# Making the transposed activations of two packs from a transposed input instead of on TensorE

## The chip, the cores and the metric

The kernel runs on one core of a Trainium2 chip. The metric is the device time of one execution in microseconds, here the median of three runs. One further execution was recorded by the hardware profiler; all the views below come from it. The core has TensorE (PE, matrix products and transposes), VectorE (DVE), ScalarE (ACT), GpSimd (POOL) and SyncE (SP), which here only issues DMA transfers.

## The reference

Two graph layers are applied to x (3327 rows of 512 features) with one weighted adjacency matrix, all in fp32. Each layer begins with a layer norm over each row, and a relu:

```
h = jnp.maximum(_layernorm(x, axis=-1), 0.0)
x = x + _L0_gnn_ref(h, adj, adj, Wq, bq, Wk, bk, Wv, bv)   # softmax(q k^T / sqrt(512) + 2 adj) v
h = jnp.maximum(_layernorm(x, axis=-1), 0.0)
x = x + _L1_gnn_ref(h, adj, W)                              # normalised adjacency, twice
```

The layer norm is (x - mean) / sqrt(variance + 1e-5), with no learned scale or offset. Because the scale of a row is positive, relu((x - mean) * rstd) equals max(x - mean, 0) * rstd. The change concerns only h of the first layer, in the stage that makes the queries.

## The kernel before, in words

The rows are padded to 26 tiles of 128. In most of the kernel the products are formed by a seven-product scheme for 2 x 2 blocks, so operands are kept as blocks and as sums of blocks. The first stage, which takes about the first 116 us, forms M = Wq^T Wk (scaled), the normalised h, its transpose, and the projection of the transposed h by M, which is stored to DRAM (`qd`) and read back by the score stage.

The 13 pairs of row tiles (tile t of the upper half and tile t of the lower half) are cut into four packs, `PACKS = ((0, 4), (4, 3), (7, 3), (10, 3))`, and the packs are worked in the order `TURN = (1, 2, 0, 3)`. Pack 0 has four pairs, so its products have 512 columns; the others have three pairs and 384 columns.

`h_transposed(k)` takes the pack's tiles one by one. `load_x` brings a tile of x from DRAM on SP's queue. `norm` computes mean and variance with bn_stats and bn_aggr on VectorE (L194, L196), adds epsilon (L198), and GpSimd raises the sum to the power -0.5 (L200, `rstd`); VectorE makes the bias -mean * rstd (L204). ScalarE applies relu(x * rstd + bias) (L323), which gives `ht`. SP stores `ht` to DRAM for later stages (L324). TensorE transposes it in four blocks of 128 x 128 into a PSUM bank of `tp` (L327). ScalarE copies the blocks into `hp[k]` (L330 for a tile of the upper half, L332 for two blocks of a lower one), and VectorE forms the block sums that need the other two blocks straight from PSUM (L333, L334). Once the pack is complete VectorE forms two more sums over all its columns (L335, L336).

`hp[k]` thus has seven parts, each of two blocks: part 0 is used by product m1, 1 by p2, 2 by p4, 3 by p5, 4 by p6, 5 by p7 and 6 by p3. The mapping is the dictionary `A`.

`project_q(k)` runs two `Chain`s, one for each half of the output features. A chain issues its seven products in the order m1, p5, p2, p6, (the p4 that the chain before left open), p3, p7 into PSUM banks X, Y and Z. ScalarE evicts some of the results into `qs` (L352), VectorE adds others to `qs` (L355), and after the second chain SP stores the four `qs` tiles to `qd` (L362). There is one set of `qs` tiles for all packs, so the next pack's evictions wait for those stores.

The order on each engine in this stage is not written out by hand: a scheduler places the instructions by its own estimate of readiness, and each engine then runs its list in that order. In the stage after it, the order is pinned by `in_order`. In the first stage the scheduler lays the transposes of a pack between the products of the pack ahead of it. The x tiles lie in a ring of eleven buffers and the `ht` tiles in a ring of four.

Of the kernel before, what the change touches and what calls it, by code (L numbers as in the profile page):

```python
# [35 lines left out]
HALF = 13  # L36
# [7 lines left out]
ROW = tuple(STRIPS[s] + y * HT[s] + k for y in range(2) for s in range(2) for k in range(HT[s]))  # L44
# [3 lines left out]
def graph_layers_kernel(  # L48
    ctx: ExitStack,
    tc: tile.TileContext,  # L50
    x: bass.AP,
    adjT: bass.AP,
    wq: bass.AP,
    wk: bass.AP,
# [22 lines left out]
    nc = tc.nc  # L77
    N = out.shape[0]
    NP, D = x.shape
    DC = D // P  # L80
    NT = NP // P
    scale = 1.0 / math.sqrt(D)
# [17 lines left out]
    def large(k, shape, name):  # L100
        return arena.tile(shape, F32, name=name, tag=f"large{k}")
# [4 lines left out]
    def half(k, shape, name):  # L106
        return arena.tile(shape, F32, name=name, tag=f"half{k}")

    def bank(k, name):
        return banks.tile([P, BW], F32, name=name, tag=f"bank{k}")  # L110

    def ring(*slots):

        turn = itertools.cycle(slots)

        def take(shape, name):
            kind, k = next(turn)
            return kind(k, shape, name)

        return take  # L120
# [18 lines left out]
    dram = ctx.enter_context(tc.tile_pool(name="dram", bufs=1, space=bass.MemoryType.DRAM))  # L139
    small = ctx.enter_context(tc.tile_pool(name="small", bufs=4))  # L140

    ident = const.tile([P, P], F32, name="ident")
# [23 lines left out]
    totd = dram.tile([1, NP], F32, name="totd")  # L166
    x1d = [dram.tile([P, D], F32, name=f"x1d{i}") for i in range(NT)]
    rowd = [[dram.tile([P, D], F32, name=f"row{g}_{i}") for i in range(NT)] for g in range(3)]
    t2d = [[dram.tile([P, 4, P], F32, name=f"t2{g}_{t}") for t in range(PAIRS + 1)] for g in range(3)]

    def four_sums(o, g):
# [16 lines left out]
        lo, hi = max(r0, c0), min(r0 + P, c0 + a.shape[-1])  # L188
        return (slice(lo - c0, hi - c0), ident[:, lo - r0 : hi - r0]) if lo < hi else None

    def norm(src):

        st = small.tile([P, 6], F32, name="st")
        nc.vector.bn_stats(st, src)  # L194
        mv = small.tile([P, 2], F32, name="mv")
        nc.vector.bn_aggr(mv, st)  # L196
        ve = small.tile([P, 1], F32, name="ve")
        nc.vector.tensor_scalar(ve, mv[:, 1:2], EPS, None, op0=ALU.add)  # L198
        rstd = small.tile([P, 1], F32, name="rstd")
        nc.gpsimd.tensor_tensor(rstd, ve, mhalf, op=ALU.pow)  # L200

        def bias():
            nb = small.tile([P, 1], F32, name="nb")
            nc.vector.scalar_tensor_tensor(nb, mv[:, 0:1], -1.0, rstd, op0=ALU.mult, op1=ALU.mult)  # L204
            return nb

        return rstd, bias
# [17 lines left out]
    def psum_ring(*ks):  # L225
        turn = itertools.cycle(ks)
        return lambda name: bank(next(turn), name)

    x_bank, y_bank, z_bank, tp_bank = psum_ring(0, 1), psum_ring(2, 3), psum_ring(4, 5), psum_ring(6, 7)
# [40 lines left out]
    x_ring = ring(*((mid, k) for k in range(6, 15)), (half, 13), (half, 14))  # L270
    n_ring = ring(*((mid, k) for k in range(4)))

    def load_x(i, queue=nc.sync):
        xt = x_ring([P, D], "xt")
        queue.dma_start(xt, x[ROW[i] * P : (ROW[i] + 1) * P])
        return xt

    order = [(k, t + y * HALF) for k in TURN for t in range(PACKS[k][0], sum(PACKS[k])) for y in range(2)]
# [29 lines left out]
    for r in range(DC):  # L308
        for z in range(2):
            turned = -scale if r < 2 and z == 0 else scale  # L310
# [5 lines left out]
    def h_transposed(k):  # L316

        a, n = PACKS[k]
        for _, i in (o for o in order if o[0] == k):
            xt = first.pop(i) if i in first else load_x(i)  # L320
            rstd, bias = norm(xt)
            ht = n_ring([P, D], "ht")
            nc.scalar.activation(ht, xt, AF.Relu, bias=bias(), scale=rstd)  # L323
            nc.sync.dma_start(rowd[0][ROW[i]], ht)  # L324
            pt = tp_bank("tp").rearrange("p (c e) -> p c e", c=DC)
            for c in range(DC):
                nc.tensor.transpose(pt[:, c], ht[:, c * P : (c + 1) * P], ident)  # L327
            w = slice((i % HALF - a) * P, (i % HALF - a + 1) * P)
            if i < HALF:
                nc.scalar.copy(hp[k][:, 0:2, :, w], pt.rearrange("p (a c) e -> p a c e", a=2))  # L330
            else:
                nc.scalar.copy(hp[k][:, 2, :, w], pt[:, 2:4])  # L332
                nc.vector.tensor_add(hp[k][:, 3, :, w], hp[k][:, 2, :, w], pt[:, 0:2])  # L333
                nc.vector.tensor_add(hp[k][:, 5, :, w], hp[k][:, 0, :, w], pt[:, 0:2])  # L334
        nc.vector.tensor_add(hp[k][:, 4], hp[k][:, 3], hp[k][:, 0])  # L335
        nc.vector.tensor_add(hp[k][:, 6], hp[k][:, 1], hp[k][:, 4])  # L336

    def project_q(k):
        a, n = PACKS[k]
        w = n * P  # L340

        qs = [half(8 + j, [P, 2, BW], "qs") for j in range(4)]

        def chain(o):
            def product(ps, name, start):
                for c in range(2):
                    nc.tensor.matmul(ps[:, :w], M[B[name]][:, c, o * P : (o + 1) * P], hp[k][:, A[name], c],  # L347
                                     start=start and c == 0, stop=c == 1, skip_group_check=True)

            def first(j, ps, sign):  # L350
                d = 2 * (j % 2) + o
                nc.scalar.activation(qs[j][:, o, :w], ps[:, :w], AF.Identity, bias=u[:, d : d + 1], scale=float(sign))  # L352

            def more(j, ps):
                nc.vector.tensor_add(qs[j][:, o, :w], qs[j][:, o, :w], ps[:, :w])  # L355

            def last():
                if o == 1:
                    for j in range(4):
                        y, z = divmod(j, 2)  # L360
                        i = ROW[y * HALF + a] * P
                        nc.sync.dma_start(qd[:, 2 * z : 2 * z + 2, i : i + w], qs[j][:, :, :w])  # L362

            Chain(product, first, more, last)

        for o in range(2):
            chain(o)
# [5 lines left out]
            nc.tensor.matmul(pu[:, r : r + 1], w_k[c // 2][:, c % 2, r * P : (r + 1) * P], bq_sb[:, c : c + 1],  # L373
                             start=c == 0, stop=c == DC - 1)
    nc.vector.tensor_scalar(u, pu[:, :DC], scale, None, op0=ALU.mult)
    for k, then in itertools.zip_longest(TURN, TURN[1:]):
        if then is not None:
            h_transposed(then)
        project_q(k)

# [144 lines left out]
    def beside_of(k):  # L525
        def on(j, what, *args):
            if 0 <= j < len(steps):
                getattr(pairs[j], what)(*args)

        def difference():  # L530
            if k < len(steps) and steps[k][1] >= 6:
                next(more_of, None)

        return (
            lambda: (on(k - 2, "s4"), on(k - 2, "gather", 0)),
            lambda: (on(k - 1, "s3"), on(k - 2, "gather", 1)),
            lambda: on(k + 1, "sum_of_adjacency", 0),
            lambda: on(k + 1, "sum_of_adjacency", 1),
            lambda: (on(k - 2, "total", 0), difference()),
            lambda: (on(k - 2, "total", 1), on(k - 1, "s1")),  # L540
            lambda: on(k - 1, "s2"),
        )
# [9 lines left out]
    with in_order(*(e.engine for e in (nc.vector, nc.tensor, nc.gpsimd, nc.sync))):  # L552
        for k, (n, t) in enumerate(steps):
# [116 lines left out]
    parts = {}  # L670
# [147 lines left out]
    class Gather:  # L818
# [14 lines left out]
        def parts(self, of):  # L833

            return [of[k][:, w] for k, w in self.spots]
# [40 lines left out]
    def where(i):  # L876

        s = int(i >= STRIPS[1])
        return (s, *divmod(i - STRIPS[s], HT[s]))
# [142 lines left out]
    def number_of(g, r, s, t):  # L1022
        return ((g * len(ORDER) + r) * 2 + s) * len(every) + t
# [18 lines left out]
    for n, job in enumerate(jobs):  # L1042
        k = k0 + n * (k1 - k0) // len(jobs)
# [15 lines left out]
    k = number_of(0, 5, 1, 2)  # L1059
# [16 lines left out]
    for (n, s, t), its in {  # L1076
# [15 lines left out]
    k = number_of(1, 4, 0, 0)  # L1092
# [480 lines left out]
```

## Time and profile before

| | us |
|---|---|
| runs shown, median of 3 | 2179.59 (2177.32 to 2180.01) |
| the profiled execution | 2178.22 |
| span of its instructions | 2176.4 |
| TensorE busy in the span | 2163.2 (99%) |
| VectorE busy | 1664.5 (76%) |
| ScalarE busy | 238.4 (11%) |
| GpSimd busy | 49.0 (2%) |
| TensorE's transposes of h (L327), busy | 16.4 |
| the products of `project_q` end, first products of the score stage | about 116 to 122 after the start |

The span is the time from the first to the last instruction. Busy time counts an engine as busy while at least one of its instructions runs; matmuls overlap, so the mean length of one is longer than the distance between two starts. In a group of instructions, what stands after the second bar is the idle time of the engine just before them and what ended it. Lines such as L327 are lines of the kernel before; where the text speaks of operations that only the changed kernel has, it goes by the names in the diff.

### The profile page before, as it was taken

How to read it: one execution, taken by the hardware profiler on the slowest of the kernel's cores; microseconds unless marked ns; L12 is line 12 of the kernel's file. 1: busy time of each engine (PE TensorE's matmuls, PEld its weight loads, DVE VectorE, ACT ScalarE, POOL GpSimd, SP SyncE). 2: the span in 40 equal slices, each digit the busy share in tenths (PEclk: the TensorE clock that was granted, in tenths of full speed). 3: DMA queues.
4: the chain of work that ended last, by engine and by line, in shares of the span. 5: the costliest groups of instructions: out<-in, count | busy, mean ns of one | idle time of the engine just before them, and what ended most of it. 6: DMA issues, size and time to landing. Idle time of an engine off the chain costs nothing.

```text
span 2176.4 us, 21093 instructions
## 1 busy us (share of the span) xinstructions
PE 2163.2 (99%) x6424; PEld 1197.1 (55%) x6424; DVE 1664.5 (76%) x3250; ACT 238.4 (11%) x363; POOL 49.0 (2%) x60
## 2 busy tenths in 40 slices
PE   9999999999999999999999999999999999999998
PEld 6555555455555555555454555555666655555555
DVE  6369888888886698886778778887676667778686
ACT  5312111121110000000000000000011100000011
POOL 2000000000000000000111000000000000000000
PEclk9999999999999999999999999999999999999999
DMA  8568888889989899888787889986646468756685
GB/s 290 177 222 308 294 298 287 294 290 310 321 290 298 291 377 331 287 296 304 259 304 263 308 277 370 320 303 219 207 145 200 142 202 276 254 188 212 218 305 194
DMA packets 300374, 583.68 MB, mean 268 GB/s; under 512 B 34518, under 2 KB 168028, under 8 KB 300252
## 3 DMA queue, kind: packets, MB, share of 16 engines
q1 hardware_dynamic: 265102, 512.76, 69.4%
q10 hardware_dynamic: 35150, 69.48, 8.7%
q8 instruction: 53, 0.87, 0.2%
q14 instruction: 69, 0.57, 0.1%
HBM read 414.28 MB, written 167.85 MB: 267 GB/s over the span
## 4 chain that ended last, share of the span: by engine, by line
PE 95%; DVE 3%; DMA 1%; issue 1%; ACT 0%; POOL 0%; DVEq 0%; POOLq 0%
PE p L813 54%; PE Y L454 13%; PE Z L454 7%; PE p L805 5%; PE p L905 4%; PE pw L966 3%; PE X L454 3%; PE Y L347 2%; PE Z L347 1%; PE mm L306 1%; DMA part<-sum 1%; PE tp L327 1%; DVE part L173 1%; PE pt L995 1%; PE X L347 0%
## 5 line engine op out<-in xcount | busy, mean ns | idle before, releaser
L813 PE MATMUL p<-part,b 128*128 128x448 f32 (+1 forms) x3528 | 1261.5, 513 | 0.3 <-DVE part L174 0.2
L813 PEld LDWEIGHTS p<-part,b 128*128 128x128 f32 x3528 | 668.1, 190 | 534.7 <-issue 284.7
L454 PE MATMUL Y<-qt,hp 128*128 128x448 f32 (+1 forms) x832 | 308.2, 513 | 0.3 <-DVE g L466 0.3
L173 DVE TENSOR_TENSOR part<-part 128x896 f32<-128x896 f32 (+1 forms) x252 | 257.0, 1020 | 65.7 <-DMA part<-p 24.0
L454 PEld LDWEIGHTS Y<-qt,hp 128*128 128x128 f32 x832 | 157.7, 190 | 134.3 <-issue 72.3
L454 PE MATMUL Z<-qt,hp 128*128 128x384 f32 (+1 forms) x416 | 162.5, 513 | 0.0
L175 DVE TENSOR_TENSOR part<-part,part 128x448 f32<-128x448 f32 (+1 forms) x219 | 129.5, 591 | 14.9
L174 DVE TENSOR_TENSOR part<-part,part 128x448 f32<-128x448 f32 (+1 forms) x219 | 129.4, 591 | 7.2
L805 PE MATMUL p<-part,b 128*128 128x448 f32 (+1 forms) x336 | 124.2, 513 | 0.0
L454 PEld LDWEIGHTS Z<-qt,hp 128*128 128x128 f32 x416 | 78.8, 190 | 67.4 <-issue 37.2
L458 DVE SCALAR_TENSOR_TENSOR g<-g,Y 128x384 f32<-128x384 f32 (+1 forms) x156 | 91.5, 587 | 31.3 <-PE Y L454 28.6
L805 PEld LDWEIGHTS p<-part,b 128*128 128x128 f32 x336 | 63.7, 190 | 53.5 <-issue 31.2
L841 ACT COPY part<-p 128x384 f32<-128x384 f32 (+1 forms) x33 | 16.6, 502 | 657.5 <-PE p L813 542.1
L454 PE MATMUL X<-qt,hp 128*128 128x384 f32 (+1 forms) x208 | 81.1, 512 | 0.0
L461 ACT ACTIVATE g<-g 128x768 f32<-128x768 f32 (+1 forms) x48 | 43.0, 896 | 347.8 <-DVE g L458 278.6
L905 PE MATMUL p<-w,ct 128*128 128x512 f32 x136 | 61.8, 594 | 0.5 <-DVE part L917 0.5
L842 DVE TENSOR_TENSOR part<-p,part 128x384 f32<-128x384 f32 (+1 forms) x33 | 19.3, 585 | 51.6 <-PE p L813 50.9
L454 PEld LDWEIGHTS X<-qt,hp 128*128 128x128 f32 x208 | 39.5, 190 | 33.1 <-issue 19.3
L200 POOL TENSOR_TENSOR rstd<-ve,mhalf 128x1 f32<-128x1 f32 x52 | 43.0, 830 | 567.9 <-DVE ve L198 538.7
L966 PE MATMUL pw<-w,rows 128*128 128x256 f32 x208 | 53.6, 380 | 0.8 <-DVE rows L956 0.8
L896 DVE TENSOR_TENSOR job<-job 128x896 f32<-128x896 f32 (+1 forms) x52 | 52.9, 1018 | 0.0
L466 DVE TENSOR_TENSOR g<-g,Z 128x384 f32<-128x384 f32 (+1 forms) x52 | 30.5, 586 | 26.8 <-PE Z L454 26.4
(176 smaller groups left out, 1697.6 us busy)
## 6 DMA issues: line engine op xcount, KB each, us to landing
part<-sum SPq DMA_DIRECT2D x104, 448.0 KB, 5.0
part<-p SPq DMA_DIRECT2D x91, 448.0 KB, 6.0
part<-sum SPq DMA_DIRECT2D x104, 384.0 KB, 3.7
part<-p SPq DMA_DIRECT2D x91, 384.0 KB, 4.4
part<-in_adjT_dram SPq DMA_DIRECT2D x78, 448.0 KB, 4.9
b<-row SPq DMA_DIRECT2D x234, 128.0 KB, 4.7
part<-in_adjT_dram SPq DMA_DIRECT2D x78, 384.0 KB, 3.5
g<-in_adjT_dram SPq DMA_DIRECT2D x52, 448.0 KB, 4.4
```

What stands on the lines that cost most here:

```text
L173: yield nc.vector.tensor_add(o[:, 0:2], g[:, 0:4:3], g[:, 1:2].to_broadcast([P, 2, g.shape[-1]]))
L174: yield nc.vector.tensor_add(o[:, 2], o[:, 1], g[:, 0])
L175: yield nc.vector.tensor_add(o[:, 3], o[:, 2], g[:, 2])
L200: nc.gpsimd.tensor_tensor(rstd, ve, mhalf, op=ALU.pow)
L347: nc.tensor.matmul(ps[:, :w], M[B[name]][:, c, o * P : (o + 1) * P], hp[k][:, A[name], c], start=start and c == 0, stop=c == 1, skip_group ...
L454: nc.tensor.matmul(ps[:, :wd], h_of(self.t, name, k), qt[B[name]][:, k], start=start and k == 0, stop=k == 1, skip_group_check=True)
L458: nc.vector.scalar_tensor_tensor(a[n], a[n], 2.0, ps[:, :wd], op0=ALU.mult, op1=ALU.add if sign > 0 else ALU.subtract)
L805: yield nc.tensor.matmul(ps[("p2", "p3", "p4", "p8")[k]][:, :w], b[:, z], a[:, 0, y], start=k == 3, stop=True)
L813: yield nc.tensor.matmul(ps[r][:, :w], b[:, i], m, start=self.t == 0, stop=self.t == PAIRS - 1 and r in ("p1", "p5", "p6", "p7"))
L896: nc.vector.tensor_add(self.a, self.a, self.b)
L905: nc.tensor.matmul(ps, cts[s][y][d][:, k * P : (k + 1) * P], w[d], start=d == 0, stop=d == DC - 1)
L966: nc.tensor.matmul(ps, a, W[B[name]][:, c], start=new and c == 0, stop=c == 1, skip_group_check=True)
```

## The change

A second copy of x, transposed, is handed to the kernel as a further input (it is laid out on the host in the same manner as the other transposed inputs). For packs 1 and 2 everything stays as it was. For packs 0 and 3, the last two in `TURN`, `h_of_transpose` takes the place of `h_transposed`:

- The tiles of x are still loaded, normalised by ScalarE and stored as `ht`, since later stages need the rows. Their mean and rstd are kept side by side in `stats` instead of in small tiles of their own.
- Four loads of the transposed x fill the parts of `hp[k]` that hold single blocks, and a tile `other` for the remaining two blocks.
- TensorE transposes the means and then the rstds of the whole pack (128 x 8 or 128 x 6 values) into one bank, ScalarE copies each to `by_row`, SP stores each to DRAM as one line (`normd`), and SP loads each line back to all 128 partitions (`norms`).
- In the transposed layout every column has its own mean and rstd, so VectorE and GpSimd subtract the mean (GpSimd for the upper half, VectorE for the lower half), VectorE applies max(x, 0) * rstd, and then it forms the four block sums. These operations are handed out one by one as `beside`, next to the evictions and additions of the pack that `project_q` is working on.

The diff, cut to its core:

```diff
-    def norm(src):
+    def norm(src, kept=None):
...
-        mv = small.tile([P, 2], F32, name="mv")
+        mv = small.tile([P, 2], F32, name="mv") if kept is None else kept
...
-        rstd = small.tile([P, 1], F32, name="rstd")
+        rstd = small.tile([P, 1], F32, name="rstd") if kept is None else kept[:, 1:2]
...
+    def h_of_transpose(k):
+        a, n = PACKS[k]
+        w = n * P
+        stats = small.tile([P, 2, 8], F32, name="stats", bufs=2)[:, :, : 2 * n]
+        for m, (_, i) in enumerate(o for o in order if o[0] == k):
+            xt = load_x(i)
+            rstd, bias = norm(xt, stats[:, :, m])
+            ht = n_ring([P, D], "ht")
+            nc.scalar.activation(ht, xt, AF.Relu, bias=bias(), scale=rstd)
+            nc.sync.dma_start(rowd[0][ROW[i]], ht)
+            if m == 2 * n - 3:
+                late = loads[-1].ins
+        other = half(2, [P, 2, BW], "a21")[:, :, :w]
+        for y in range(2):
+            c0 = ROW[y * HALF + a] * P
+            xs = xT[:, c0 : c0 + w].rearrange("(z c p) e -> z p c e", z=2, p=P)
+            for z, to in enumerate((hp[k][:, 0], hp[k][:, 1]) if y == 0 else (other, hp[k][:, 2])):
+                ins = nc.sync.dma_start(to, xs[z]).ins
+                tc.add_manual_dep(ins, late.name,
...
+        pt = tp_bank("tp")
+        by_row = half(3, [P, P], "by_row")
+        everywhere = []
+        for m in range(2):
+            nc.tensor.transpose(pt[: 2 * n, m * P : (m + 1) * P], stats[:, m], ident)
+            rows = by_row[32 * m : 32 * m + 2 * n]
+            nc.scalar.copy(rows, pt[: 2 * n, m * P : (m + 1) * P])
+            to = normd[k][m][:, : 2 * w]
+            nc.sync.dma_start(to[0].rearrange("(i p) -> i p", p=P), rows)
+            everywhere.append(half(m, [P, 2 * BW], "norms")[:, : 2 * w])
+            nc.sync.dma_start(everywhere[m], to[0:1].to_broadcast([P, 2 * w]))
+        mean, by = ([e.rearrange("p (t y e) -> p t y e", t=n, y=2)[:, :, y] for y in range(2)] for e in everywhere)
+
+        def parts():
+            for y, four in ((0, (hp[k][:, 0, 0], hp[k][:, 0, 1], hp[k][:, 1, 0], hp[k][:, 1, 1])),
+                            (1, (hp[k][:, 2, 0], hp[k][:, 2, 1], other[:, 0], other[:, 1]))):
+                for block in four:
+                    v = block.rearrange("p (t e) -> p t e", t=n)
+                    yield (nc.vector if y else nc.gpsimd).tensor_sub(v, v, mean[y])
+                    yield nc.vector.scalar_tensor_tensor(v, v, 0.0, by[y], op0=ALU.max, op1=ALU.mult)
+            yield nc.vector.tensor_add(hp[k][:, 3], hp[k][:, 2], other)
+            yield nc.vector.tensor_add(hp[k][:, 5], hp[k][:, 0], other)
+            yield nc.vector.tensor_add(hp[k][:, 4], hp[k][:, 3], hp[k][:, 0])
+            yield nc.vector.tensor_add(hp[k][:, 6], hp[k][:, 1], hp[k][:, 4])
+
+        return parts()
...
-    def project_q(k):
+    def project_q(k, beside):
...
                 nc.scalar.activation(qs[j][:, o, :w], ps[:, :w], AF.Identity, bias=u[:, d : d + 1], scale=float(sign))
+                next(beside, None)
...
                 nc.vector.tensor_add(qs[j][:, o, :w], qs[j][:, o, :w], ps[:, :w])
+                for _ in range(2):
+                    next(beside, None)
...
-    for k, then in itertools.zip_longest(TURN, TURN[1:]):
-        if then is not None:
-            h_transposed(then)
-        project_q(k)
+    h_transposed(TURN[1])
+    for n, k in enumerate(TURN):
+        parts = h_of_transpose(TURN[n + 1]) if 1 <= n < 3 else iter(())
+        project_q(k, parts)
+        for _ in parts:
+            pass
```

More of the change, by code (lines that the diff above doesn't have):

```diff
@@ L51, in graph_layers_kernel @@
     x: bass.AP,
+    xT: bass.AP,
     adjT: bass.AP,
@@ L168, in graph_layers_kernel @@
     rowd = [[dram.tile([P, D], F32, name=f"row{g}_{i}") for i in range(NT)] for g in range(3)]
+    normd = {k: [dram.tile([1, 2 * 4 * P], F32, name=f"norm{m}_{k}") for m in range(2)] for k in range(4)}
     t2d = [[dram.tile([P, 4, P], F32, name=f"t2{g}_{t}") for t in range(PAIRS + 1)] for g in range(3)]
@@ L271, in graph_layers_kernel @@
     n_ring = ring(*((mid, k) for k in range(4)))
+    loads = []
     def load_x(i, queue=nc.sync):
         xt = x_ring([P, D], "xt")
-        queue.dma_start(xt, x[ROW[i] * P : (ROW[i] + 1) * P])
+        loads.append(queue.dma_start(xt, x[ROW[i] * P : (ROW[i] + 1) * P]))
         return xt
@@ L336, in h_transposed @@
         nc.vector.tensor_add(hp[k][:, 6], hp[k][:, 1], hp[k][:, 4])
-    def project_q(k):
+    def h_of_transpose(k):
[17 more added lines that the diff above has]
+                tc.add_manual_dep(ins, late.name,
+                                  mybir.DependencyInfo(mybir.DependencyClass.NoSync, mybir.DependencyReason.DATA),
+                                  reason="in_order")
+        pt = tp_bank("tp")
[22 more added lines that the diff above has]
+        return parts()
@@ L1549 @@
         "x": padded(x),
+        "xT": turned(padded(x)),
         "adj": plain(adj),
@@ L1567 @@
             bad = flag.tile([1, 1], mybir.dt.int32, name="bad")
-            x_in, adj_in, *rest = args
-            with tc.If(graph_layers_kernel(tc, x_in, *rest, out, bad) > 0):
+            x_in, xT_in, adj_in, *rest = args
+            with tc.If(graph_layers_kernel(tc, x_in, xT_in, *rest, out, bad) > 0):
                 general_kernel(tc, x_in[: x.shape[0]], adj_in, *rest, out)
```

## The prediction

> **What bounds the kernel now.** I read the page's busy shares first, then its chain of waits, then the stage that the change touches: the groups by form up to 105 us, TensorE's timeline there, and busy time by stretches.
>
> ```profile
> PE 2163.2 (99%) x6424; PEld 1197.1 (55%) x6424; DVE 1664.5 (76%) x3250; ACT 238.4 (11%) x363; POOL 49.0 (2%) x60
> ...
> PE 95%; DVE 3%; DMA 1%; issue 1%; ACT 0%; POOL 0%; DVEq 0%; POOLq 0%
> ```
>
> TensorE is busy 99% of the span and carries 95% of the chain that ended last: work that leaves it is worth its full time, unless a wait takes the place.
>
> ```profile
> L327 PE MATMUL tp<-ident,ht 128*128 128x128 f32 x104 | 16.4, 296 | 0.8 <-ACT hp L330 0.7
> ...
> L330 ACT COPY hp<-tp 128x512 f32<-128x512 f32 x13 | 7.6, 582 | 9.3 <-PE tp L327 9.3
> ...
> L333 DVE TENSOR_TENSOR hp<-hp,tp 128x256 f32<-128x256 f32 x13 | 5.4, 416 | 6.4 <-ACT hp L332 6.4
> L334 DVE TENSOR_TENSOR hp<-hp,tp 128x256 f32<-128x256 f32 x13 | 5.4, 414 | 0.0
> ```
>
> The 104 transposes (26 row tiles of four) overlap, so their price is not 296 ns. It is read from starts in TensorE's timeline (start, length, then what):
>
> ```profile
> 49.17 1.04 PE L327 MATMUL tp<-ident,ht 128*128 128x128 f32 x8
> 50.05 0.81 PE L347 MATMUL Y<-hp,M 128*128 128x384 f32 x2
> 50.69 0.60 PE L327 MATMUL tp<-ident,ht 128*128 128x128 f32 x4
> 51.13 0.81 PE L347 MATMUL Y<-hp,M 128*128 128x384 f32 x2
> ...
> 81.89 0.59 PE L347 MATMUL Z<-hp,M 128*128 128x512 f32 x1
> ```
>
> Eight cost 0.88 us, four 0.44. Products follow without a gap: two records (one fp32 matmul, 384 columns) take 0.645 us, one of 512 columns 0.86.
>
> Busy time by stretches (PE, PEld, DVE, ACT, POOL, then clock, DMA share, GB/s):
>
> ```profile
> 24.00:25.00 1.00, 0.97 (x5) 0.57 (x4) 0.53 (x4) 0.00 (x0) 0.00 (x0) 0.51 0.64 225
> 25.00:26.00 1.00, 0.35 (x2) 0.35 (x3) 0.00 (x0) 0.99 (x2) 0.00 (x0) 0.50 0.05 18
> ...
> 40.00:50.00 10.00, 10.00 (x40) 6.22 (x39) 9.92 (x29) 3.49 (x7) 0.84 (x2) 1.00 0.75 250
> 50.00:60.00 10.00, 9.86 (x48) 6.53 (x47) 5.46 (x20) 10.00 (x20) 3.29 (x6) 1.00 0.71 261
> 60.00:70.00 10.00, 10.00 (x32) 5.89 (x31) 3.42 (x5) 2.77 (x5) 0.00 (x0) 1.00 0.30 108
> 70.00:80.00 10.00, 10.00 (x43) 5.84 (x42) 4.71 (x10) 5.03 (x10) 0.00 (x0) 1.00 0.94 313
> 80.00:90.00 10.00, 10.00 (x25) 4.56 (x24) 4.26 (x7) 2.92 (x5) 0.00 (x0) 1.00 0.61 213
> ```
>
> TensorE has no slack from 31 us on; VectorE is half free from 50 to 90, the cover that the change draws on.
>
> ```profile
> row<-ht SPq DMA_DIRECT2D x26, 256.0 KB, 2.4
> ...
> g<-in_adjT_dram SPq DMA_DIRECT2D x6, 384.0 KB, 4.2
> ```
>
> DMA up to 125 us, median from issue to landing: a store 2.4 us, a load 4.2.
>
> [...] No run here shows a POOL operation wider than 128 elements. [...] The trace's 0.50 at 25 us, after narrow matmuls and a wait, [...] it lasts to 30.5 us.
>
> **The change, part by part.** I use the order of the changed program's instructions and the durations above.
>
> *TensorE.* 14 tiles of transposes go: at their starts 3.53 us for pack 0, 2.64 for pack 3, and a 0.29 us wait for a bank at 54.6; together 6.46. Four transposes of statistics come, 0.11 each. The ceiling is 6.0 us; other parts can only take from it.
>
> *ScalarE.* 14 copies go (7 x 0.58 + 7 x 0.37 = 6.7 us), four small ones come. No cost: the copies that go fill much of ScalarE's 10.00 us of 10 from 50 to 60.
>
> *VectorE.* Pack 0: four pairs L333/L334 go (4 x 0.83 = 3.3 us); four subtractions and eight max-times operations of 512 columns come at 0.69 (the 128x512 rows of L918 and L312), and two wide additions at 1.22: +7.4 us. Pack 3: -2.5 + 12 x 0.55 + 2 x 0.95 = +6.0. The free half covers the sum; its place is the question.
>
> *DMA.* Eight loads of xT (3.7 MB), four stores of statistics (4 and 3 KB), four broadcasts (1.8 MB): 5.5 MB, 14 us at 384 GB/s, against some 17 us of idle share from 40 to 90 us. The broadcast of bv at 648.7 us ran in stretches of 313 to 384 GB/s, so a repeated source isn't slow; I price one like a load, 4 us ([...] up to 6).
>
> *The new chain, pack 0.* The first statistics transpose stands at the end of project_q of pack 1, 49.2 us, the second one matmul later. The statistics are ready: the last rstd of pack 0 ended at 46.1 before. Copies to by_row end at 49.8 and 50.5, the mean's store lands at about 52 [...]. SP's queue waits for that, then issues the broadcasts: mean and rstd land at about 56.5 and 58. Behind SP's wait stand the qd stores that free qs for pack 2: ScalarE then reads p5 at about 59.5, and TensorE needs that at 61.8: 2 us of slack. VectorE's queue stands at the first subtraction from 54 to 56.5; behind it are its additions to qs, which TensorE needs first at 63.7. The x loads of pack 3 move behind all this on SP's queue, from 43 us to 56 to 58.5; they land by 63 and are read from 67 on, so they are covered, as are pack 3's rstd on POOL's queue, which stand behind its subtractions (61.7) and are wanted from 74 on.
>
> From 56.5 VectorE has: three subtractions (58.6); five max-times, three of them held by POOL's subtractions at 1.3 us each, [...] (63.1; with 2.2 each, 66.5); addition Y to qs (63.7, TensorE unhurt); then X 0.55, two max-times 1.4, Z 0.55, subtraction, max-times and two statistics 2.9, Z 0.55, the addition for part 3: 70.8. TensorE, without the transposes that stood ahead of its p5 at 75.0, wants part 3 at 69.3: **stall 1.5**. Then Y 0.55, two additions 2.44, two small ones, one addition: 75.3; four more bn_stats with their aggregates and small ones, 4.4: 79.8. TensorE's next statistics transpose, for pack 3, waits for the last aggregate; it gets there at 77.3: **stall 2.5**. TensorE takes up p3 of pack 0 at about 80.0, against 81.89 before.
>
> *The new chain, pack 3.* The second transpose stands two products later, 83.4. Stores 84.0, broadcasts at about 89.5 and 90.3 (0.8 MB of qt and adjacency ahead). Three subtractions, seven max-times with POOL's at 1.0 us, another subtraction and max-times, two additions to qs and three of parts end at 101. TensorE needs part 4 at 100.4: **stall 0.6**. Behind SP's wait for these stores stand stores of pack 0 and adjacency loads of the next stage, which begins at 115: covered.
>
> *Sum.* 6.0 - 1.5 - 2.5 - 0.6 = 1.4; a gain of **1.4 us**. The later order of all engines is as before, so the rest shifts whole. Against the profiled execution, 2178.22 (span 2176.4 and 1.8 around it), that is 2176.8. It stands 1.4 below the median of the runs shown, 2179.59, so the median to expect is **2178.2**.
>
> *Bounds.* A broadcast landed at 3 us instead of 4, and POOL at 0.9 us: stalls shrink by 2 to 3.5. A broadcast at 6, or POOL at 2.2: each adds about 2 to 3 us in each pack, since VectorE's list has no gap in which to make it up.
>
> **Rivals.** What a measurement of this kernel can tell from no change is about 0.2%, 4.4 us.
>
> *Covered (0.55, likeliest).* As worked out: transposes gone, most of their time turned into waits for VectorE. Own range 2175.5 to 2182, all within 0.2%.
>
> *Chain early (0.15).* Mean at 54, statistics transposes unhurt: stalls at most 1.5, gain 4.5 to 5.5, about 2174.8. For it: VectorE half free, ceiling 6.0. [...]
>
> *Slower: TensorE stalls and its clock halves (0.3).* Place: the first statistics transpose of pack 3, at 77 us, queued in order ahead of products that could run. Price: [...] the clock falls to 0.50, as at 24.5 to 30.5 us, where 6 us at half speed cost 3. With norms 2 us late and POOL at 2.2, stalls are 4 to 5 for pack 0 beyond forecast, 2 for pack 3, plus 3: 6 to 9 us lost net, 2184 to 2187. For it: VectorE at 9.92 of 10 us just before, DMA at 0.94 in 70 to 80. Against: three late things together.
>
> *The change does nothing.* Excluded: the order has 56 transposes fewer.
>
> **How the numbers follow.** Faster by over 0.2%: the early case, 0.15. Slower by over 0.2%: the third, 0.3. Between: 0.55. The range reaches from the early case's 2174.5 to 2186.
>
> **What would show it.** Right: 48 row-tile transposes in tp and four of stats; TensorE's first waits after 50 us at part 3 of pack 0, then 2 to 3 us at the statistics transpose near 77; norms landing 4 us after issue. Wrong: norms before 55 us or after 59, POOL subtractions over 2 us, clock under 1.0 after 50 us, or TensorE waiting at qs.

## The result, and the profile after

The changed kernel takes 2184.62 us (median; 2183.1 to 2187.43) against 2178.76 of the kernel before (2175.35 to 2181.49) in the same comparison: a ratio of 1.0027, interval 1.0019 to 1.0034. It is **slower by 5.9 us**, where a gain of 1.4 us (a median of 2178.2) was forecast. Its profiled execution took 2186.5 us, with a span of 2184.4.

The page's busy shares and its chain of waits, after:

```profile
PE 2161.3 (99%) x6372; PEld 1191.3 (55%) x6372; DVE 1683.5 (77%) x3264; ACT 233.9 (11%) x353; POOL 60.0 (3%) x68
...
PE 89%; DVE 5%; DMA 5%; issue 1%; SPq 0%; ACT 0%; POOL 0%; DVEq 0%; ACTq 0%
```

TensorE issues 52 instructions fewer (56 transposes out, 4 in), and GpSimd's eight new subtractions are there. TensorE's share of the chain fell from 95% to 89%. That is not the size of the loss: 6% of the span is some 130 us, and most of the long DMA pieces on the new chain lie behind 500 us. The chain took another way; what was lost has to be read in the stage itself.

The groups by form up to 105 us (line, engine, operation, count, then busy time and mean ns):

```profile
L331 PE MATMUL tp<-ident,ht 128*128 128x128 f32 x48 | 8.6, 324 | 0.7 <-ACT hp L334 0.7
...
L383 POOL TENSOR_TENSOR hp<-hp,norms 128x512 f32<-128x512 f32 x4 | 6.8, 1728 | 13.5 <-DMA norms<-norm 13.5
...
L369 PE MATMUL tp<-ident,stats 128*8 128x128 f32 x2 | 0.5, 273 | 0.0
L369 PE MATMUL tp<-ident,stats 128*6 128x128 f32 x2 | 0.5, 270 | 0.3 <-DVE stats L198 0.3
```

So the change did what it says: 48 transposes of row tiles are left of 104. Where the time went shows in TensorE's timeline (start, length, what, then the idle time before it and its releaser). First the score stage's first product in the kernel before, then the changed kernel:

```profile
115.82 1.45 PE L454 MATMUL Y<-qt,hp 128*128 128x384 f32 x4
```

```profile
55.69 4.14 PE L401 MATMUL Y<-hp,M 128*128 128x384 f32 x12 [1.22 <-ACT qs L406]
...
67.59 2.39 PE L401 MATMUL Y<-hp,M 128*128 128x384 f32 x4 [2.60 <-DVE qs L410]
...
81.92 0.27 PE L369 MATMUL tp<-ident,stats 128*6 128x128 f32 x1 [0.34 <-DVE stats L198]
...
98.67 0.91 PE L401 MATMUL Y<-hp,M 128*128 128x384 f32 x2 [0.28 <-DVE hp L384]
...
103.15 1.12 PE L401 MATMUL Y<-hp,M 128*128 128x512 f32 x2 [2.27 <-DVE qs L410]
105.85 3.76 PE L401 MATMUL Y<-hp,M 128*128 128x384 f32 x10 [0.27 <-DVE hp L387]
...
119.78 0.49 PE L513 MATMUL Y<-qt,hp 128*128 128x384 f32 x1
```

The last of these lines is the first product of the score stage. It is **4.0 us later** than before, and everything lost up to there was lost between 49 and 106 us. The two large waits are for `qs`: TensorE has a bank to write and an addition of VectorE has not yet read it.

By stretches (PE, PEld, DVE, ACT, POOL, then the clock, DMA share, GB/s):

```profile
50.00:60.00 10.00, 8.78 (x28) 4.87 (x27) 2.67 (x3) 2.46 (x5) 2.07 (x2) 1.00 0.92 312
60.00:70.00 10.00, 7.40 (x21) 4.04 (x20) 10.00 (x13) 1.63 (x3) 4.72 (x3) 0.91 0.93 318
70.00:80.00 10.00, 10.00 (x24) 4.78 (x24) 9.39 (x19) 3.31 (x5) 2.08 (x2) 0.92 0.36 119
...
100.00:110.00 10.00, 7.46 (x21) 3.39 (x20) 8.20 (x14) 2.67 (x5) 0.00 (x0) 1.00 0.66 223
```

After the wait that ends at 67.59 the clock is at half for about 3.4 us, which is what 0.91 and 0.92 over ten microseconds each amount to (0.9 + 0.8 = 1.7 us of TensorE's work lost).

Why VectorE's addition was late: its timeline and GpSimd's, from the landing of the means and scales on.

```profile
57.88 2.37 DVE L383 TENSOR_TENSOR hp<-hp,norms 128x512 f32<-128x512 f32 x2 [1.65 <-DMA norms<-norm]
60.17 1.75 DVE L383 TENSOR_TENSOR a<-a,norms 128x512 f32<-128x512 f32 x1
61.84 5.23 DVE L384 SCALAR_TENSOR_TENSOR hp<-hp,norms 128x512 f32<-128x512 f32 x5
67.00 0.54 DVE L410 TENSOR_TENSOR qs<-qs,Y 128x384 f32<-128x384 f32 x1
...
69.59 0.68 DVE L383 TENSOR_TENSOR a<-a,norms 128x512 f32<-128x512 f32 x1
```

```profile
57.93 6.80 POOL L383 TENSOR_TENSOR hp<-hp,norms 128x512 f32<-128x512 f32 x4 [13.48 <-DMA norms<-norm]
```

While GpSimd's four subtractions run (57.93 to 64.73), VectorE's own subtraction of 512 columns takes up to 1.76 us; the same subtraction at 69.59, with GpSimd idle, takes 0.68. Eight wide operations stand ahead of the addition to `qs` at 67.00; they took 9.1 us. Four of the eight are slowed, two subtractions and two max-times. Some of them taken singly, GpSimd's between VectorE's:

```profile
59.66 1.71 POOL L383 TENSOR_TENSOR hp<-hp,norms 128x512 f32<-128x512 f32 x1
60.17 1.75 DVE L383 TENSOR_TENSOR a<-a,norms 128x512 f32<-128x512 f32 x1
61.34 1.71 POOL L383 TENSOR_TENSOR hp<-hp,norms 128x512 f32<-128x512 f32 x1
61.84 1.75 DVE L384 SCALAR_TENSOR_TENSOR hp<-hp,norms 128x512 f32<-128x512 f32 x1
```

They end at 61.37, 61.92, 63.05 and 63.59: each of VectorE's 0.55 us after one of GpSimd's, and each of GpSimd's 1.12 us after one of VectorE's. The two engines take turns. VectorE doesn't wait for data here: it shows no idle time between 57.88 and 67.00, and its slowed subtractions use nothing that GpSimd made.

### The profile page after: what moved, and what is told of

Read it like the earlier page. It is cut to its first block, busy times and chain, and to the rows that moved or that the text cites. A ratio compares the mean times of both kernels' runs of the same rounds, so it can differ in the third digit from the quotient of the medians.

```text
span 2184.4 us, 21018 instructions
## 1 busy us (share of the span) xinstructions
PE 2161.3 (99%) x6372; PEld 1191.3 (55%) x6372; DVE 1683.5 (77%) x3264; ACT 233.9 (11%) x353; POOL 60.0 (3%) x68
## 4 chain that ended last, share of the span: by engine, by line
PE 89%; DVE 5%; DMA 5%; issue 1%; SPq 0%; ACT 0%; POOL 0%; DVEq 0%; ACTq 0%
PE p L872 51%; PE Y L513 13%; PE Z L513 6%; PE p L864 5%; PE p L964 3%; PE pw L1025 3%; PE X L513 3%; DMA rows<-row 2%; PE Y L401 1%; DVE part L175 1%; PE mm L310 1%; DMA part<-sum 1%; DMA sum<-job 1%; PE Z L401 1%; PE pt L1054 1%
## 5 line engine op out<-in xcount | busy, mean ns | idle before, releaser
L401 PE MATMUL Y<-hp,M 128*128 128x384 f32 (+1 forms) x128 | 51.8, 535 | 6.6 <-DVE qs L410 4.9
```

## The experiments

**Theories.** A, *slowing*: GpSimd and VectorE slow each other while both work on the parts, VectorE's additions to `qs` come late, and TensorE's wait and half clock follow. B, *the way through DRAM*: stores and broadcasts of the statistics land too late, whichever engine subtracts. C, *the qs stores*: further transfers on SP's queue keep `qs` occupied, and ScalarE's evictions wait. In what follows "first product" is the start of the score stage's first product in the profiled execution (115.82 before, 119.78 after); it is of one execution each, and how far it varies between executions was not measured. Every ratio is against the kernel before on the same chip.

| kernel | first product, us | median, us (before) | ratio, interval |
|---|---|---|---|
| the change | 119.78 | 2184.62 (2178.76) | 1.0027, 1.0019 to 1.0034 |
| no_pool | 112.98 | 2178.39 (2179.43) | 0.9994, 0.9985 to 1.0002 |
| only_0 | 120.03 | 2182.54 (2179.43) | 1.0012, 1.0005 to 1.0019 |
| only_3 | 117.48 | 2178.46 (2179.43) | 0.9997, 0.9988 to 1.0006 |
| only_0_np | 114.23 | 2177.78 (2179.07) | 0.9996, 0.9989 to 1.0002 |
| only_3_np | 113.30 | 2176.47 (2179.41) | 0.9986, 0.9979 to 0.9993 |
| known_norms | 119.61 | 2184.04 (2179.43) | 1.0018, 1.0011 to 1.0025 |
| bare | 114.20 | 2179.93 (2179.41) | 0.9998, 0.9990 to 1.0005 |
| early_np | 118.45 | 2183.69 (2179.41) | 1.0020, 1.0013 to 1.0028 |
| only_3_early_np | 114.72 | 2178.17 (2179.41) | 0.9992, 0.9986 to 0.9999 |
| no_transposes | 108.97 | 2172.95 (2179.07) | 0.9972, 0.9962 to 0.9981 |
| late | 119.70 | 2182.93 (2179.07) | 1.0012, 1.0006 to 1.0019 |

### no_pool: all subtractions on VectorE

```diff
-                    yield (nc.vector if y else nc.gpsimd).tensor_sub(v, v, mean[y])
+                    yield nc.vector.tensor_sub(v, v, mean[y])
```

> The eight subtractions of GpSimd (four of each changed pack) go to VectorE; all else as in the changed kernel. Measure: start of the score stage's first product (115.8 us before, 119.8 changed). Theory 1 (GpSimd and VectorE slow each other [...]: the subtractions took 1.0 to 1.75 us on both engines): each subtraction falls to about 0.69 us at 512 columns and 0.55 at 384, the wait of 2.6 us at 65 us shrinks, and the score stage starts 1.5 to 3 us earlier, 117 to 118. Rival (the late statistics alone set the loss, no slowing): VectorE has 4 x 0.69 + 4 x 0.55 = 5.0 us more to do in a list without a gap, and the score stage starts 2 to 5 us later, 122 to 125.

VectorE's timeline, with GpSimd out of it:

```profile
58.11 1.90 DVE L383 TENSOR_TENSOR hp<-hp,norms 128x512 f32<-128x512 f32 x3 [2.49 <-DMA norms<-norm]
59.92 1.89 DVE L384 SCALAR_TENSOR_TENSOR hp<-hp,norms 128x512 f32<-128x512 f32 x3
61.73 1.29 DVE L383 TENSOR_TENSOR hp<-hp,norms 128x512 f32<-128x512 f32 x2
62.93 0.55 DVE L410 TENSOR_TENSOR qs<-qs,Y 128x384 f32<-128x384 f32 x1
```

Again eight wide operations lie between the landing and the addition to `qs`. They take 4.8 us instead of 9.1, although VectorE now does work that GpSimd did. The norms landed at 58.1, no earlier than in the change. TensorE's waits and the first product:

```profile
55.09 4.14 PE L401 MATMUL Y<-hp,M 128*128 128x384 f32 x12 [0.46 <-ACT qs L406]
71.34 1.98 PE L401 MATMUL Z<-hp,M 128*128 128x512 f32 x4 [0.45 <-DVE hp L385]
80.14 0.27 PE L369 MATMUL tp<-ident,stats 128*6 128x128 f32 x1 [0.38 <-DVE stats L198]
98.03 1.13 PE L401 MATMUL Y<-hp,M 128*128 128x512 f32 x2 [0.75 <-DVE qs L410]
112.98 1.46 PE L513 MATMUL Y<-qt,hp 128*128 128x384 f32 x4
```

No wait over 0.75 us is left, the clock stays at 1.00 from 40 to 120 us, and the first product is 6.8 us earlier than in the change. One word of the source undoes the whole loss: theory A. Some 0.8 us of the 6.8 don't come from the slowing, though: the first wait was already shorter (0.46 for 1.22) before any subtraction began. The way through DRAM is unchanged here, so B by itself doesn't make the loss.

### only_0 and only_3: one pack at a time, GpSimd as in the change

```diff
 # only_0
-        parts = h_of_transpose(TURN[n + 1]) if 1 <= n < 3 else iter(())
+        parts = iter(())
+        if n == 1:
+            parts = h_of_transpose(TURN[2])
+        if n == 2:
+            h_transposed(TURN[3])
 # only_3 has h_transposed(TURN[2]) at n == 1 and parts = h_of_transpose(TURN[3]) at n == 2
```

> Only pack 0 is made from the transposed x; pack 3 keeps its transposes. Ceiling for pack 0: 3.53 + 0.29 - 0.22 = 3.6 us. In the changed kernel the waits up to 75 us were 1.2 (qs stores), 2.6 (addition Y) and some 1.7 for the halved clock, 5.5 together. If they belong to pack 0 alone, the score stage starts at about 115.8 - 3.6 + 5.5 = 117.7. If half of the loss needs pack 3's loads and statistics in VectorE's list, it starts at 115 to 116.5.

> Only pack 3 is made from the transposed x; pack 0 keeps its transposes. Ceiling for pack 3: 2.64 us of transposes less two statistics transposes, 2.4 us. If the losses of pack 3 (2.3 us at p4 of pack 0, 0.6 at its own parts) come from pack 0 having made everything late (its x loads wait on SP behind pack 0's statistics), they go, and the score stage starts at 113.5 to 114.5, 1.5 to 2.3 us before the kernel before. If pack 3's own chain is what is late, the waits stay and it starts at 115.5 to 117.

Pack 0 alone puts the first product at 120.03, 4.2 us late, against an expected 117.7. The rows of tile `norms` (duration min/median/max) and TensorE's timeline of only_0:

```profile
L383 POOL TENSOR_TENSOR hp<-hp,norms x4: 1704/1710/1772, 58.1 to 63.2; 128x512 f32<-128x512 f32 x4
L383 DVE TENSOR_TENSOR hp<-hp,norms x2: 693/1226/1758, 58.1 to 58.7; 128x512 f32<-128x512 f32 x2
```

```profile
62.03 1.56 PE L401 MATMUL Z<-hp,M 128*128 128x384 f32 x4 [1.22 <-ACT qs L406]
67.78 2.93 PE L401 MATMUL Y<-hp,M 128*128 128x384 f32 x4 [3.54 <-DVE qs L410]
```

The wait is 3.54 us, and the clock is at half for 6.8 us (0.83 and 0.82 in the two stretches from 60 to 80 us). The half clock begins at 66.70, in the wait, so 2.9 us of TensorE's work are lost on top. Pack 3 alone has no wait before 95 us, but one then, for another engine:

```profile
95.48 4.97 PE L401 MATMUL Y<-hp,M 128*128 128x512 f32 x8 [2.13 <-ACT qs L406]
```

```profile
94.01 0.84 ACT L471 ACTIVATE qt<-qt 128x768 f32<-128x768 f32 x1 [6.80 <-DVE qt L182]
94.76 1.25 ACT L406 ACTIVATE qs<-Y,u 128x512 f32<-128x512 f32 x2
```

The second fence is ScalarE's timeline. In its list a scaling of `qt` (L471), work of the next stage, stands ahead of the eviction. It waits for VectorE, which had slowed operations up to 84.3, the rest of the pack's up to 92.5, and then 0.47 us of waiting for `qt` itself. So the price of a slower VectorE is paid through ScalarE here. The 2.13 us were followed by 3.4 us of half clock too (0.83 from 90 to 100 us).

### only_0_np and only_3_np: the same, with all subtractions on VectorE

The edit of no_pool, on only_0 and only_3.

> Pack 0 alone made from the transposed x, all subtractions on VectorE. With them on GpSimd pack 0 alone put the first product of the score stage at 120.0 and the total 3 us above before. If GpSimd and VectorE slowing each other is what loses: first product near 114 to 115.8, total -1.5 to 0. If the way of the statistics through DRAM or the qs stores lose on pack 0: near 118 to 120 again, total +2 to +4.

> Only pack 3 from the transposed x, as in the earlier run, but its subtractions on VectorE. Slowing [...] predicts: the list from 78.7 to 92.5 us (13.8 us with GpSimd) gets about 2 us shorter although VectorE does four more operations, and the wait of 2.1 us behind it shrinks to under 0.7; the score stage starts at 113.5 to 114.5 instead of 117.5. Without slowing VectorE has 2.2 us more to do, the wait grows to 3 to 4 us and the start is 118 or later.

Without GpSimd's subtractions the first product comes much earlier for each pack: pack 0 from 120.03 to 114.23 (5.8 us), pack 3 from 117.48 to 113.30 (4.2 us). Tile `norms` in only_3_np:

```profile
L383 DVE TENSOR_TENSOR hp<-hp,norms x6: 549/551/559, 78.1 to 83.4; 128x384 f32<-128x384 f32 x6
L384 DVE SCALAR_TENSOR_TENSOR hp<-hp,norms x6: 549/550/552, 79.5 to 84.9; 128x384 f32<-128x384 f32 x6
```

Every operation takes its undisturbed 0.55 us. For pack 0 the norms came at the same time in both runs (58.07 and 58.05), so the difference is the slowing. For pack 3 the slowing is only a part: VectorE's list, 13.85 us in only_3 (78.65 to 92.50), became 0.75 us shorter (78.12 to 91.22, though four subtractions and an addition to `qs` had come into it), not 2 us as expected; the norms also landed 0.5 us earlier, and the wait of 0.47 us for `qt` was gone. only_3_np keeps 2.5 us of the 2.64 that pack 3's transposes cost in front, and its total is 2.9 us below before. It is **faster than both kernels**, by 0.14% against before (0.07 to 0.21%); of the other versions with all their computation only only_3_early_np is clear of before too, by 0.08% (0.01 to 0.14%).

### known_norms: the broadcasts need not wait for the statistics

Constant lines are stored at the start and broadcast; the statistics are stored to lines that nobody reads. The scale and mean applied to packs 0 and 3 are thus not the rows' own.

```diff
+            nc.sync.dma_start(unread[k][m][:, : 2 * w][0].rearrange("(i p) -> i p", p=P), rows)
-            nc.sync.dma_start(to[0].rearrange("(i p) -> i p", p=P), rows)
...
+        nc.vector.memset(given, float(m))
+        for k in (0, 3):
+            nc.scalar.dma_start(normd[k][m], given)
```

> The broadcasts read lines of zeros (mean) and ones (rstd) that are stored to DRAM in the first microseconds, so nothing waits for the statistics; statistics, their transposes and their stores stay, into lines that nobody reads. In packs 0 and 3 the projected and scored h is therefore relu(x) without the layer norm. If the statistics' way through DRAM sets the loss: VectorE starts on pack 0 some 6 us earlier, no wait over 0.5 us is left, and the score stage starts at 110 to 111.5. If slowed subtractions or full VectorE set it: they still take 1.2 to 1.7 us each, and the start stays above 114.

The first product stayed at 119.61. But this kernel does not isolate B, because the scheduler used the freedom: TensorE now waited 2.59 us (for `qs` by ScalarE, at 51.5), 1.47 (the same, at 61.1) and 2.88 (the statistics transpose at 80.18), with 3.4 us of half clock after the last. So it shows that early norms alone don't bring the gain, not that their way costs nothing. What it does give is GpSimd's price where VectorE doesn't hold it up:

```profile
L384 POOL TENSOR_TENSOR hp<-hp,norms x8: 995/1136/1276, 45.4 to 78.9; 128x512 f32<-128x512 f32 x4, 128x384 f32<-128x384 f32 x4
```

1.27 us for 512 columns and 1.0 for 384. With VectorE at work beside it GpSimd took 1.70 to 1.77 for 512. And it shows who waits for whom, on a VectorE operation of one column:

```profile
48.40 0.16 DVE L207 SCALAR_TENSOR_TENSOR nb<-stats 128x1 f32<-128x1 f32 x1 [3.55 <-POOL stats L203]
48.92 1.21 DVE L207 SCALAR_TENSOR_TENSOR nb<-stats 128x1 f32<-128x1 f32 x1 [0.36 <-POOL stats L203]
```

The second began 0.08 us after a subtraction of GpSimd (48.84 to 50.11) and ended 0.02 us after it: 1.21 us for work of 0.16. Both operands that it reads lie in SBUF, one value for each partition. A bn_stats of 512 columns, with one operand, took its usual 0.66 us at 76.58 while GpSimd subtracted.

### bare: only the loads of the transposed x, and the sums

No statistics transposes, broadcasts, subtractions or max-times for packs 0 and 3: h is left as the transposed x.

```diff
-            nc.tensor.transpose(pt[: 2 * n, m * P : (m + 1) * P], stats[:, m], ident)
...
-                    yield (nc.vector if y else nc.gpsimd).tensor_sub(v, v, mean[y])
-                    yield nc.vector.scalar_tensor_tensor(v, v, 0.0, by[y], op0=ALU.max, op1=ALU.mult)
```

> Left out: in packs 0 and 3 the transposed h is the transposed x itself, with no mean, no rstd and no relu; the statistics' transposes, the stores and broadcasts and the 32 subtract and max-times operations are gone. Loads of xT and the block sums stay. This is the ceiling: what the whole change could bring if its new chain cost nothing. The score stage starts at 115.8 - 6.4 = 109.4 us or up to 1 us later. If time gained in the first stage passes through to the end, the ratio to the kernel before is 0.9970 (6.4 of 2179). If the end of the score stage waits for DMA at a set distance (in the kernel without GpSimd 2.8 us were gained and a wait of 3.0 stood at 632 us), the ratio is 0.9985 to 0.9995, and the wait for g at 625 to 635 us is 4 to 6 us.

It was expected to show the ceiling and did not: the first product came at 114.20. From ScalarE's waits (in total, times, longest) and TensorE's timeline:

```profile
ACT qs L387 <- DMA qd<-qs: 16.0, 2, 8.3
```

```profile
75.45 4.97 PE L382 MATMUL Y<-hp,M 128*128 128x512 f32 x8 [2.98 <-ACT qs L387]
```

ScalarE waited up to 8.3 us for the stores that free `qs`, and TensorE behind it 1.86 us at 53.4 and 2.98 at 75.4, with 3.4 us of half clock after the second. This is theory C. no_transposes, below, leaves out the same transposes but has no transfers of xT: there ScalarE waits 1.7 us at most for these stores, and TensorE never behind it. In the change C is the first wait, 1.22 us.

### early_np and only_3_early_np: pack 3's statistics asked for earlier

With the subtractions on VectorE, the statistics of pack 3 are formed one pack earlier (in early_np together with pack 0's), and the scheduler then places their transposes and stores earlier too.

```diff
+        if n == 1:
+            seen = [h_of_transpose(t) for t in TURN[2:]]
+        if 1 <= n < 3:
+            parts = rest_of_transpose(TURN[n + 1], *seen[n - 1])
```

> Both packs from the transposed x, subtractions on VectorE, and the loads and statistics of pack 3 asked for together with those of pack 0, so that its lines are in DRAM some 20 us before they are wanted. If pack 3's late statistics cost what was left in the kernel without GpSimd (waits of 0.4 at 80 us and 0.75 at 98 us), the score stage starts at 111 to 112.5 against 113.0 there. Rival: VectorE and DMA are fuller just when pack 0 is wanted, pack 0 waits longer, and it starts at 113.5 to 116.

> Only pack 3 from the transposed x, subtractions on VectorE, its loads and statistics asked for one pack earlier. Ceiling 2.4 us. If the slowed subtractions and ScalarE's place behind qt (a wait of 2.1 us at 95 us with only pack 3 changed) were the loss, the score stage starts at 113.4 to 114.2 and no wait over 0.5 us is left. Rival: ScalarE's copy of qt still stands in front of evictions and waits for VectorE: start at 115 to 117.5, with a wait of about 2 us at 93 to 96.

TensorE's timeline in early_np:

```profile
63.22 0.37 PE L374 MATMUL tp<-ident,stats 128*6 128x128 f32 x1 [4.66 <-ACT by_row L376]
```

The transposes of statistics stand in order in TensorE's list, so a small one that is held up stops all products behind it. This one waits for ScalarE's copy of the transpose before it, and that copy waited 7.3 us for `by_row`, the buffer from which pack 0's statistics were still being stored. TensorE lost 4.66 us, and the clock was at half for 6.8 us from 62.82 on: 118.45, later than either expectation. A statistics transpose in TensorE's way was the prediction's third rival; it loses here and in known_norms (2.88 us), not in the change itself, where it waits 0.34 us. only_3_early_np, in which `h_of_transpose(TURN[3])` is called one turn earlier and pack 0 is as before, has its first product at 114.72, 1.4 us behind only_3_np; TensorE waits 1.12 us for ScalarE in it, so its expectation (114.2 at most, no wait over 0.5) was missed.

### no_transposes and late: do microseconds of the first stage count in full?

The kernel before, once with the transposes of packs 0 and 3 left out, once with 3.9 us of repeated products put in; neither adds a transfer.

```diff
 # no_transposes
+            if k in (0, 3):
+                pt = ht.rearrange("p (c e) -> p c e", c=DC)
+            else:
 # late
-                for c in range(2):
+                for c in tuple(range(2)) * (4 if (k, o, name) == (3, 1, "m1") else 1):
```

> The kernel before with TensorE's transposes of packs 0 and 3 left out: ScalarE's copies and VectorE's sums read ht itself in place of the bank, so h of these packs is not transposed; no transfer is added. This is the ceiling of the change by itself. By the first-stage sum 6 us less: first product of the score stage near 110, total -6 if all after it shifts. If late transfers near 630 us set the end of the score stage, part of the 6 comes back there as a wait of TensorE: total -2 to -4.

> The kernel before, with the first product of pack 3's second half issued four times instead of once: 6 more matmuls of 384 columns, 0.645 us each, so 3.9 us more of TensorE work in the first stage and no other change, transfers included. First product of the score stage at 119.7. If everything after the first stage simply shifts: +3.9 us. If the transfers that are late near 630 us in the score stage set that stage's end: +0 to +2.

TensorE's timeline at the score stage's first product, in no_transposes and then in late:

```profile
108.97 1.45 PE L457 MATMUL Y<-qt,hp 128*128 128x384 f32 x4
```

```profile
119.70 1.45 PE L454 MATMUL Y<-qt,hp 128*128 128x384 f32 x4
```

6.85 us earlier gave 6.1 us less in all (by the ratio's interval 4.1 to 8.3), and 3.9 later gave 3.9 more by the medians (1.3 to 4.1 by the interval). So the rest shifts nearly whole, both ways, and the ceiling was there to be had.

## Why the prediction was wrong

**Right: the ceiling.** 6.0 us net of the statistics transposes; no_transposes with four times 0.11 added gives 6.4. Right, too, was that VectorE's list has no gap in which to make anything up.

**Right in number by luck.** The 2184.6 lies within the third rival's 2184 to 2187, and a wait followed by half a clock was its mechanism. But its sum was another: norms 2 us late, GpSimd at 2.2 us, and TensorE stopped at the statistics transpose. The means came 1.4 us late, GpSimd took 1.77, and at that transpose TensorE waited only 0.34. Of the signs of being wrong, two showed (clock under 1.0 after 50 us, TensorE waiting at `qs`) and two did not (norms outside 55 to 59, GpSimd's subtractions over 2 us).

**The step that failed: VectorE's list of pack 0, "three subtractions (58.6); five max-times, three of them held by POOL's subtractions at 1.3 us each" (63.1).** The order came as forecast, three subtractions and then five max-times. But any slowing was put on GpSimd's side of the sum only, and as a delay of data. Its 1.3 us was the author's estimate; no trace of before showed an operation of GpSimd that wide. It is about what GpSimd takes alone (1.27 in known_norms); beside VectorE it took 1.70 to 1.77. And VectorE's own operations, priced at 0.69 throughout, took up to 1.76 in the same time. By these lengths one after the other would be 1.27 + 0.69 = 1.96 us for a pair (an estimate from known_norms and the kernel before). The change's trace is near it: the two engines' operations end in turn, a pair every 1.68 us, so only some 0.3 us of a pair ran in parallel. The list up to the addition Y, 6.6 us in the prediction (56.5 to 63.1), took 9.1 (57.88 to 67.00), and without the slowing 4.8 (no_pool).

That addition thus began 3.9 us late: 2.5 by the list and 1.4 by the landing of the means. Their broadcast was issued at 51.94, as forecast, but took 5.9 us, not some 4. The late landing alone does no harm: in no_pool the norms land at 58.1 and TensorE doesn't wait for Y. Together with the slowing it makes up about half of the wait of 2.60 us (an estimate from these figures; no run has the slowing with an earlier landing and the same order). Upper bounds for GpSimd (2.2 us) and for a broadcast (6 us) were there, at 2 to 3 us each; the first covered GpSimd's own operations, not VectorE's.

**The other terms.**
- *qs stores.* The "2 us of slack" was for the read of p5, behind the broadcasts: it came at 61.39 for 59.5, and TensorE didn't stop for it. The wait came earlier, where the prediction had no term: ScalarE's first eviction of pack 2 stood until 55.06 for a store issued at 50.65, ahead of the broadcasts, and TensorE stood 1.22 us behind it. That store took some 4.4 us to land, with xT loads in flight; the stores of `qs` in the kernel before took 2.6 (median from 40 to 64 us).
- *Pack 3.* The second statistics transpose came at 85.46 for 83.4, and the subtractions began at 93.0 for 89.5: broadcasts issued at 87.8 took 5.2 us instead of 4. With slowed operations after that, TensorE waited 2.27 us for an addition to `qs` where no stall was forecast, and 0.28 and 0.27 for parts of `hp`, for 0.6 forecast.
- *The stalls that were forecast* at part 3 of pack 0 (1.5) and at the statistics transpose (2.5) shrank to none and 0.34, since TensorE itself came later.

**The clock.** How long a stall must be to halve it, no trace of before showed. 2.60 us did in the change, 2.13 in only_3; yet 2.59 us at 51.5 in known_norms and 2.27 at 103 in the change did not. Within each trace the clock changes at whole multiples of 3.41 us from each other (in the change half for 6.83, full for 37.55, half for 3.41). So TensorE's idle time can be counted in windows of that length (length, PE busy, PEld, DVE, ACT, POOL, clock, DMA share, GB/s):

```profile
64.77:68.18 3.41, 0.81 (x3) 0.46 (x3) 3.41 (x7) 0.58 (x1) 0.00 (x0) 1.00 0.98 362
98.90:102.31 3.41, 1.98 (x6) 0.82 (x5) 3.41 (x8) 0.58 (x1) 0.00 (x0) 1.00 0.07 24
102.31:105.73 3.42, 2.43 (x6) 0.97 (x6) 3.42 (x6) 0.00 (x0) 0.00 (x0) 1.00 0.85 263
```

The wait of 2.60 us lies in one window; that of 2.27 lies across an edge, so that the two windows have 1.4 and 1.0 us of idle time. In all thirteen traces, from 31 to 2160 us, each of the eight windows at full clock with 2.13 us or more of idle time was followed by half a clock, and none with 1.70 or less. The half clock went on for a second window where TensorE was still idle for 1.1 or 1.3 us in the first (only_0, early_np), and not where it was idle for 0.4 or less. (Before 31 us the clock also fell: in the kernel before at 24.0, after a window full of products of one column, and ahead of the wait at 25.0, of 0.68 us, that the prediction named beside them.)

**The sum as measured**, up to the first product: from no_transposes' 108.97 to the change's 119.78 it is 10.8 us. Six waits are 6.98; each moves the next start by about 0.17 more than is listed, since the list counts from a modelled end (in no_pool, a product due at 53.17 + 1.29 began at 55.09, 0.63 later, for 0.46 listed), 1.0 in all; the half clock is 1.7, the statistics transposes 0.44. That leaves 0.7 us to small things.

**What stays open.** In the profiled executions the span grew by 8.0 us (by the medians it is 5.9): 4.0 before the score stage's first product and 4.0 behind it. There TensorE's and SP's instructions come in the same order as before (from 140 us on); the lists of VectorE and ScalarE differ in a few places. From the first product to the end the change and its variants with both packs (no_pool, known_norms, bare, early_np) take 2063.7 to 2066.2 us of their profiled executions; all others, before among them, 2060.6 to 2062.4. In the former, TensorE waits 2.3 to 3.9 us near 525 and 635 us, at the end of the score stage, where the DMA share is 0.7 to 1.0; in the others 0 to 1.7. In no_pool and bare the last of these waits also halved the clock for 3.4 us. TensorE's waits from 500 to 660 us in no_pool, and then in the kernel before:

```profile
PE Y L513 <- DVE g L525: 3.0, 1, 3.0
```

```profile
PE Y L454 <- DVE g L466: 0.3, 1, 0.3
```

So no_pool, 2.8 us ahead at its first product, ends only 1.0 ahead. late has the change's first product without its transfers, and does not have the loss, so lateness as such is not its cause. Whether the transfers of two packs leave something behind for a place 400 us later was not shown; the cause stays open.

## What to carry to other kernels

Before work is split between GpSimd and VectorE, price the instructions of *both* for the time that they overlap; here, with two SBUF operands for each of VectorE's, a pair took 1.68 us for 0.69 and 1.27 alone, so the two lists were better counted one after the other, and giving all of it to VectorE was the faster split (4.8 us for 9.1 up to the addition to `qs`). In an engine's list, look up what stands behind the slowed instruction (here the additions that free PSUM banks), because that is where TensorE stops. A variant that leaves the removed work out, with nothing put in its place, tells the ceiling, and one with a known delay put in tells whether a microsecond of the stage counts in full.

## What was not expected of the hardware

- A two-operand fp32 subtraction of 128 x 512 took 0.68 us on VectorE alone and 1.27 on GpSimd alone (known_norms). When both had one, 1.76 and 1.71 to 1.77: they took turns, a pair every 1.68 us. Even a VectorE operation of one column, with two SBUF operands, took 1.21 us for 0.16 when GpSimd's subtraction had just begun.
- TensorE's clock went to half after each window of 3.41 us in which TensorE was idle for 2.13 us or more, and after none with 1.70 or less. So a stall of 2.13 us halved it in only_3, and one of 2.59 in known_norms, across the edge of two windows, did not.
